# Issuing ScalarE's copy of the row-end column one group of turns sooner

## The chip, the cores and the metric

The kernel runs on one core of a Trainium2 chip. The time is the device time of one execution in microseconds (us); the kernel before has a median of 2385.87 us over three runs (2383.38 to 2386.52). The profile is one further execution, taken by the hardware profiler. Its engines are TensorE (PE, its weight loads PEld), VectorE (DVE), ScalarE (ACT), GpSimd (POOL) and SyncE (SP), which here issues nearly all DMAs.

## The reference, cut to what matters

The input x has 8 images (batches) of 256 channels and 96 x 96 pixels, float32. Two layers are added to it one after the other, each behind a group norm.

```python
def layer0(x):                          # w1, w2, w3, w_out: 256x256, 8 heads of 32 channels
    q, k, v = (fft2(pconv(x, w, b)) for w, b in ((w1, b1), (w2, b2), (w3, b3)))
    q, k = l2_normalize(q), l2_normalize(k)         # over the 9216 frequencies
    attn = einsum('bhcn,bhdn->bhcd', q, k) * temperature
    attn = complex(softmax(real(attn)), softmax(imag(attn)))
    return pconv(abs(ifft2(einsum('bhcd,bhdn->bhcn', attn, v))), w_out)

def layer1(x):                          # q, k: 32 channels, v: 256
    q, k, v = softplus(Wq x + bq), softplus(Wk x + bk), Wv x + bv
    return q (k^T v) / (q . sum(k))     # linear attention over the 9216 pixels

x = x + layer0(gn(x))
x = x + layer1(gn(x))
```

No Fourier transform is needed for the attention's logits. Their real part is a sum over pixels of products of x with itself, and their imaginary part a sum of products of x with x mirrored (row h with row H - h, column w with column W - w). The kernel forms both from the even and odd parts e = f + g and o = f - g, where f is a pixel and g its mirror image.

## The kernel before, in words

The order of work is written out by hand: inside `tc.manual_schedule` every engine executes its instructions in the order in which the program issues them. So an instruction that waits holds up all that stands behind it on its engine.

Each batch goes through these stages. `pair_sums(b)` makes the sums of products of batch b. `attention(b)` makes 36 mixing columns from them. `rotate(b)` transforms rows. `images(b)` makes, for 24 chunks of 384 pixels, the heads' images and projects them into x. `layer1(b)` and `output(b)` are the second layer. The stages of two batches are woven: while `images(b)` works on its last chunks (15 to 23) and `layer1(b)` runs, `pair_sums(b + 1)` is advanced step by step (`weave`). The first sums of batch 0 are made by other code, and its groups 3 to 5 are not woven with images.

In `images`, chunk i takes: the products z on TensorE (L898), an addition of two tables on VectorE (L945), squares on ScalarE (L949), their sum on GpSimd (L950), square roots on ScalarE (L951, and L952 for eight rows of another tile), the projection po of chunk i - 2 on TensorE (L907), its addition to x on VectorE (L909) and two statistics (L313). Every eighth chunk has a few more (L929, L931, L932). Both `images` and `pair_sums` take their working tiles from one ring of five.

`pair_sums` goes over row pairs u = 0 to 12, two of them to a group v = u // 2; a group is one load. Loads alternate between two staging areas (`staged(b, v)`, with index v % 2), each with a part f and a mirrored part g. A turn, `turn_blocks(u)`, makes two 32x32 block transposes on VectorE (L514, one of f and one of g, 128 x 768 each) into `turned(b, u)`, which holds both turns of a group. The columns of g are read backwards from one row's end; the pixel of column 0 has to stand at that end. For this the even turn (r == 0) begins with a copy on ScalarE (L510) that shifts 16 elements on each of the 128 partitions by one row width within g. The second transpose waits for it.

After the odd turn of group v, SP issues two stores of the turned group to DRAM (L520) and the load of group v + 2 into the area that has come free (`load_grouped`, L169 and L171, eight DMAs of 192 KB). The stores read what the turns wrote, and the next group's turns write over it.

`pair(u)` makes the tile eo of e and o from the two transposes: a small memset (L530), the sum (L542, GpSimd) and the difference (L543, VectorE for even u, GpSimd for odd u in batches 1 to 7; pair 0 is made on VectorE). `products` (L475) then runs three sets of matmuls over each eo. During pair u, at its first set, pair u + 1 is made, and at its second set turn u + 2:

```python
if q == 0 and u < NG and u + 1 not in ready:
    prepare(("pair", u + 1), lambda u=u: make(u + 1))
if q == 1 and u + 2 <= NG:
    prepare(("turn", u + 2), lambda u=u: turn_blocks(u + 2))
```

Turns 0 and 1 and pairs 0 and 1 are made together at the start, at chunk 15 of the images. `prepare` runs a step at once, except for turns 10, 11 and 12 and pair 10 in batches 1 to 7: these are held, and `layer1` and `output` release them piece by piece (`release`). `layer1` starts with a group norm: VectorE's L329, ScalarE's L331 and L337, VectorE's L339, with small TensorE products (L128) between, then scaled weights (L975) and the products of L1020.

Of the kernel before, what the change touches and what calls it, by code (L numbers as in the profile page):

```python
# [74 lines left out]
def two_layer_kernel(ctx: ExitStack, tc: tile.TileContext, x, w1t, b1, w2t, b2, w3, b3, wot, temp,  # L75
                     wqt, bq, wkt, bk, wvt, bv, gavg, gmat, tmat, out):
    nc = tc.nc
    B, C, H, W = x.shape
# [11 lines left out]
    NG = H // 2 // G  # L90
# [17 lines left out]
    def x_of(b):  # L108
        return arenas[b % 2]
# [4 lines left out]
    def acc_tile(name):  # L114
        return pacc.tile([P, 512], F32, tag="acc", name=name)

    def ring_tile(name):
        return ring.tile([P, 2 * NQ * (C + 2)], F32, tag="ring", name=name)
# [14 lines left out]
    SG = NB8 * 2 * W  # L133
# [4 lines left out]
    def staged(b, v, at=0):  # L138

        return x_of(b)[:, v % 2, at * SG:at * SG + SG + at]  # L140

    def turned_flat(b, u):

        if b == 0 and u // 2 in (V0 + 1, NG // 2):
            return y_of(b)[:, :, TO2:TO2 + 2 * NQ * C]
        return x_of(b)[:, :, TO:TO + 2 * NQ * C]

    def turned(b, u):

        t = turned_flat(b, u)  # L150
        return [t[:, c].rearrange("p (q r n) -> p q r n", q=NQ, r=2) for c in range(2)]

    def load_grouped(b, v):

        xs = x[b].rearrange("(c i) h w -> i c h w", i=32)
        if 2 * v == NG:
            m = H // 2
            f, g = (staged(b, v, i)[:, 0:C].rearrange("p (c w) -> p c w", c=NB8) for i in range(2))
            for q in range(NQ):
                s = slice(32 * q, 32 * q + 32)  # L160
                n = 32 if q else 31
                o = W + 1 - 32 * (q + 1)
                nc.sync.dma_start(out=f[s], in_=xs[:, :, m, s])
                nc.sync.dma_start(out=g[s, :, 0:n], in_=xs[:, :, m, o:o + n])
            return
        f, g = (staged(b, v, i)[:, 0:SG].rearrange("p (c w) -> p c w", c=NB8) for i in range(2))
        for a in range(G):
            h, s = 2 * (G * v + a), slice(32 * a, 32 * a + 32)
            nc.sync.dma_start(out=f[s], in_=xs[:, :, h:h + 2].rearrange("p c r w -> p c (r w)"))  # L169
            if h:  # L170
                nc.sync.dma_start(out=g[s], in_=xs[:, :, H - h - 1:H - h + 1].rearrange("p c r w -> p c (r w)"))  # L171
            else:
                nc.sync.dma_start(out=g[s, :, 0:W], in_=xs[:, :, H - 1])
                nc.sync.dma_start(out=g[s, :, W:2 * W], in_=xs[:, :, 0])
# [170 lines left out]
    def finish(stage):  # L345
        for _ in stage:
            pass
# [109 lines left out]
    def weights(b):  # L457

        return ring_tile(f"wl_{b}")[:, 0:6 * C].rearrange("p (k o) -> p k o", k=KC)

    def products(acc, eo, q, np_, first, last):
        for c in range(2):
            v = eo[0:np_, q, c]
            for m in range(4):
                if m == 3:
                    to, of = C + 2, bass.AP(v.tensor, v.offset, [list(v.ap[0]), [C - HP + 1, 2], [1, HP + 1]])
                    n = 2 * (HP + 1)
                else:
                    to, n = ((0, 3 * HP + 1), (HP + 1, 3 * HP + 1), (C + 3, P + 1))[m] if not first else ((0, C + 2), (0, C + 2), (C + 2, P + 2))[m]
                    lo = to - (m // 2) * (P + 2)  # L470
                    of = v[:, lo:lo + n]
                o = acc[c][m % 2 * HP:m % 2 * HP + HP, to:to + n]
                if m == 3:
                    o = o.rearrange("p (f n) -> p f n", f=2)
                nc.tensor.matmul(o, lhsT=v[:, 1 + m * HP:1 + (m + 1) * HP], rhs=of, start=(first and m < 2), stop=last,  # L475
                                 skip_group_check=True)

    def pair_sums(b):

        ready = {}  # L480
        u0 = 0 if b else 2 * V0

        def prepare(key, step):
            if b and key in (("turn", 10), ("pair", 10), ("turn", 11), ("turn", 12)):
                held[key] = step()
            else:
                finish(step())

        def make(u):
            ready[u] = pair(u)  # L490
            yield

        acc = [acc_tile(f"acc{c}_{b}") for c in range(2)] if b else s0[0]
        CB = C + 2

        def turn_blocks(u):

            v, r = divmod(u, 2)
            t = turned(b, u)
            if u == NG:  # L500
                f, g = (staged(b, v, i)[0:W, 0:C].rearrange("p (c w) -> p c w", c=NB8) for i in range(2))
                nc.vector.tensor_copy(g[0:32, :, 31:32], f[0:32, :, 0:1])
                for i, src in enumerate((f, g[:, :, ::-1])):
                    nc.vector.transpose(out=t[i][0:W, 0, 0].rearrange("p (c i) -> p c i", c=NB8), in_=src)
                nc.sync.dma_start(out=xtm, in_=t[0][0:W, 0, 0])
                return
            f = staged(b, v, 0).rearrange("p (c r w) -> p c r w", c=NB8, r=2)
            if r == 0:
                g = staged(b, v, 1)
                nc.scalar.copy(g[:, SG:0:-W], g[:, SG - W::-W])  # L510
            o = SG + (1 - r) * W + 1
            g = x_of(b)[:, v % 2, o:o + SG].rearrange("p (c n) -> p c n", c=NB8)[:, :, W - 1::-1]
            for i, src in enumerate((f[:, :, r], g)):
                nc.vector.transpose(out=t[i][:, :, r].rearrange("p q (c i) -> p q c i", c=NB8),  # L514
                                    in_=src.rearrange("p c (q w) -> p q c w", q=NQ))
                if i == 0:
                    yield 1
            if r:
                for c in range(2):
                    nc.sync.dma_start(out=xtd[v][:, :, c], in_=turned_flat(b, u)[:, c].rearrange("p (q m) -> p q m", q=NQ))  # L520
                if v + 2 <= NG // 2:
                    load_grouped(b, v + 2)

        def pair(u):

            eo = ring_tile(f"eo_{b}_{u}").rearrange("p (q c n) -> p q c n", q=NQ, c=2)
            nq, np_ = (NQ, P) if u < NG else (1, W)
            ft, gt = (t[0:np_, 0:nq, u % 2] for t in turned(b, u))
            e, o = (eo[0:np_, 0:nq, c, 1:C + 1] for c in range(2))
            (nc.gpsimd if u < NG else nc.vector).memset(eo[0:np_, 0:nq, :, 0:CB:CB - 1], 1.0 if u < NG else R2)  # L530
            if u == 0:
                nc.gpsimd.memset(eo[0:32, 0:nq, :, 0:CB:CB - 1], R2)
            if u in (0, NG):
                w = R2 if u else pw
                if u:
                    nc.scalar.activation(o, gt, AF.Copy, scale=w)
                else:
                    nc.vector.tensor_scalar_mul(o, gt, w)
                nc.vector.scalar_tensor_tensor(e, in0=ft, scalar=w, in1=o, op0=ALU.mult, op1=ALU.add)
                nc.vector.scalar_tensor_tensor(o, in0=ft, scalar=w, in1=o, op0=ALU.mult, op1=ALU.subtract)  # L540
            else:
                nc.gpsimd.tensor_add(e, ft, gt)  # L542
                (nc.gpsimd if b and u % 2 and u < NG - 1 else nc.vector).tensor_sub(o, ft, gt)  # L543
            return eo, nq, np_

        for step in (turn_blocks(u0), make(u0), turn_blocks(u0 + 1)):
            finish(step)
            if b == 0:
                yield
        finish(make(u0 + 1))  # L550
        yield
        for u in range(u0, NG + 1):
            eo, nq, np_ = ready.pop(u)
            for q in range(nq):
# [4 lines that stand above are left out]
                if (u, q) == (NG - 1, 1):  # L559
                    wl = weights(b)  # L560
                products(acc, eo, q, np_, u == 0 and q == 0, u == NG)
                yield
        s0[b] = acc, wl
# [678 lines left out]
    E = mybir.EngineType  # L1242
    with tc.manual_schedule(engines={E.PE, E.DVE, E.Pool, E.SP, E.Activation}):
        sums, rest, loads, parts = first_sums(), pair_sums(0), first_loads(), tables()
        fetch, turns, tables_to = rotate(0)
        next(loads)
# [81 lines left out]
```

## Time and profile before

| | |
|---|---|
| median of three runs | 2385.87 us |
| the profiled execution | 2381.32 us |
| its span, first to last instruction | 2379.5 us |
| TensorE busy | 2322.5 us, 98% |
| VectorE busy | 1731.4 us, 73% |
| ScalarE busy | 1154.2 us, 49% |
| GpSimd busy | 854.5 us, 36% |
| granted TensorE clock, mean | 0.996 |
| DMA traffic | 405.10 MB, 170 GB/s |
| L510, the copy | 45 times, median 220 ns |
| L514, the transposes | 180 times, median 967 ns |

How to read the lines below. A row of the page's list of groups has the line in the code, the engine and operation, the tiles written and read, the count, then the busy time and the mean duration in ns, and after the bar the idle time of the engine before these instructions, with what ended most of it. A row of the list of waits has who waited for whom, the total in us, how often, and the longest. A row of a timeline has the start and the duration in us, the engine, line, operation, tiles, count (TensorE's counts include its weight loads), and in square brackets the idle time before it and what ended it. An engine with a "q" behind it (DVEq, ACTq, SPq) is that engine's sequencer, which waits and issues.

### The profile page before, as it was taken

To read this page: it belongs to the slowest core of one execution; us is meant where nothing else is said; L and a number is where in the kernel's file an instruction comes from. 1 tells how busy PE (TensorE), PEld (TensorE's weight loads), DVE (VectorE), ACT (ScalarE), POOL (GpSimd) and SP (SyncE) were. 2 spreads that over 40 slices of the span, in tenths; PEclk is the share of its full clock that TensorE was granted. 3 is DMA by queue.
4 is the path that set the end of the run, shared out by engine and by line. 5 is a ranking of instruction groups with operands and counts; after the bars stand their busy time and mean duration, and the time that the engine had idled before them with its cause. 6 is when DMAs were issued, how large, how long until landed. Compare 5 with 4: busy or idle time off the path is not lost. (4 is left out here: it accounts for less than half of the span.)

```text
span 2379.5 us, 62270 instructions
## 1 busy us (share of the span) xinstructions
PE 2322.5 (98%) x26028; PEld 1440.0 (61%) x26028; DVE 1731.4 (73%) x3392; ACT 1154.2 (49%) x2052; POOL 854.5 (36%) x810
## 2 busy tenths in 40 slices
PE   9999999999999999999999999999999999999997
PEld 7844667456674566745666457664676546765444
DVE  5577786777867777677776778767786777876776
ACT  2354454544545355454554535445364453644563
POOL 5234513344223443234341353413524245142412
PEclk9999999999999999999999999999999999999999
DMA  9735749177591666926577364863759538584004
GB/s 252 210 121 145 187 139 331 59 172 174 164 336 41 161 160 203 312 50 159 138 250 264 67 170 132 281 211 67 194 135 292 173 94 195 146 276 179 1 8 160
DMA packets 280346, 405.10 MB, mean 170 GB/s; under 512 B 39363, under 2 KB 202595, under 8 KB 280067
## 3 DMA queue, kind: packets, MB, share of 16 engines
q1 hardware_dynamic: 279714, 401.05, 58.2%
q8 instruction: 206, 3.38, 0.6%
q14 instruction: 74, 0.60, 0.1%
q0 software_dynamic: 352, 0.08, 0.1%
HBM read 251.90 MB, written 149.14 MB: 169 GB/s over the span
## 5 line engine op out<-in xcount | busy, mean ns | idle before, releaser
L898 PE MATMUL z<-arena,mz 128*64 128x384 f32 (+1 forms) x3840 | 593.1, 487 | 0.6 <-issue 0.6
L950 POOL TENSOR_TENSOR e<-e 128x768 f32<-128x768 f32 x192 | 349.3, 1819 | 539.7 <-ACT e L949 513.0
L907 PE MATMUL po<-e,wo 128*64 128x384 f32 x3072 | 529.7, 486 | 2.9 <-ACT e L951 1.7
L898 PEld LDWEIGHTS z<-arena,mz 128*64 128x64 f32 (+1 forms) x3840 | 247.7, 131 | 295.0 <-issue 284.8
L907 PEld LDWEIGHTS po<-e,wo 128*64 128x64 f32 x3072 | 228.2, 137 | 268.6 <-issue 232.2
L945 DVE TENSOR_TENSOR e<-z,xT 128x768 f32<-128x768 f32 x384 | 357.6, 946 | 43.4 <-PE z L898 43.2
L949 ACT ACTIVATE e<-e 128x1536 f32<-128x1536 f32 x192 | 284.4, 1481 | 160.5 <-DVE e L945 158.7
L475 PE MATMUL acc<-eo 128*64 128x193 f32 (+4 forms) x4448 | 341.4, 303 | 13.1 <-POOL eo L542 11.7
L475 PEld LDWEIGHTS acc<-eo 128*64 128x64 f32 (+1 forms) x4448 | 301.4, 136 | 81.5 <-issue 46.7
L951 ACT ACTIVATE e<-e 128x768 f32<-128x768 f32 x192 | 162.0, 844 | 381.5 <-POOL e L950 379.5
L909 DVE TENSOR_TENSOR arena<-arena,po 128x384 f32<-128x384 f32 x384 | 208.0, 549 | 149.9 <-PE po L907 149.8
L128 PE MATMUL y<-tm,arena 96*64 96x97 f32 x6144 | 300.3, 249 | 10.9 <-issue 3.4
L128 PEld LDWEIGHTS y<-tm,arena 96*64 96x64 f32 x6144 | 274.4, 137 | 58.4 <-issue 36.5
L542 POOL TENSOR_TENSOR eo<-arena 128x768 f32<-128x768 f32 x83 | 172.4, 2077 | 345.2 <-DVE arena L514 244.8
L1213 POOL TENSOR_TENSOR arena<-arena,po 128x384 f32<-128x384 f32 x180 | 179.2, 1016 | 279.3 <-ACT po L1212 278.4
L514 DVE STREAM_TRANSPOSE arena<-arena 128x768 f32<-128x768 f32 x180 | 170.2, 962 | 98.6 <-ACT arena L510 83.7
L313 DVE BATCH_NORM_STATS2 st<-arena 128x6 f32<-128x384 f32 x384 | 195.0, 547 | 0.5
L838 ACT COPY arena<-y 128x384 f32<-128x384 f32 (+1 forms) x200 | 94.7, 476 | 155.1 <-PE y L128 141.3
L838 DVE COPY arena<-y 128x384 f32<-128x384 f32 (+1 forms) x192 | 104.1, 543 | 77.2 <-PE y L128 73.7
L1065 PE MATMUL xT<-ident,arena 128*128 128x128 f32 x1152 | 144.1, 275 | 1.3 <-ACT xT L1068 1.3
L1065 PEld LDWEIGHTS xT<-ident,arena 128*128 128x128 f32 x1152 | 127.1, 141 | 19.0 <-issue 16.5
L1212 ACT COPY po<-o 128x384 f32<-128x384 f32 x180 | 80.1, 483 | 101.5 <-PE o L128 87.1
(255 smaller groups left out, 2475.8 us busy)
## 6 DMA issues: line engine op xcount, KB each, us to landing
arena<-in_x_dram SPq DMA_DIRECT2D x99, 768.0 KB
out_dram<-arena SPq DMA_DIRECT2D x192, 384.0 KB
xtd<-arena SPq DMA_DIRECT2D x90, 768.0 KB
arena<-xtd SPq DMA_DIRECT2D x180, 384.0 KB
arena<-in_x_dram SPq DMA_DIRECT2D x353, 192.0 KB
tm<-rx SPq DMA_DIRECT2D x96, 159.0 KB
wl<-in_w1t_dram SPq DMA_DIRECT2D x8, 256.0 KB
wl<-in_w2t_dram SPq DMA_DIRECT2D x8, 256.0 KB
```

What stands on the lines that cost most here:

```text
L128: nc.tensor.matmul(out[h], lhsT=lhsT[:, h], rhs=rhs, start=start, stop=stop, skip_group_check=True)
L313: nc.vector.bn_stats(out=st[:, k, c, :], in_=x_of(b)[:, k, c * CH:(c + 1) * CH])
L475: nc.tensor.matmul(o, lhsT=v[:, 1 + m * HP:1 + (m + 1) * HP], rhs=of, start=(first and m < 2), stop=last, skip_group_check=True)
L838: copy(y[:, :, :, g:g + nr, :], v.rearrange("p k r (f w) -> p k f r w", f=2))
L898: nc.tensor.matmul(out[:, 0:CH].rearrange("p (h q) -> p h q", q=PR), lhsT=columns(mz, k, c, j)[:, h], rhs=yz[:, k, f, :, o:o + PR], start= ...
L907: nc.tensor.matmul(po[h, 0:CH], lhsT=wo[:, k, m * P:(m + 1) * P][:, h], rhs=e[:, k, :], start=(k == 0), stop=(k == KC - 1), skip_group_che ...
L909: nc.vector.tensor_add(x[:, m, n], x[:, m, n], po[:, 0:CH])
L945: nc.vector.tensor_add(e[:, 2 * c:2 * c + 2, :].rearrange("p t (q h) -> p t q h", h=H), pz[:, 0:CH].rearrange("p (h q) -> p q h", h=H).uns ...
L949: nc.scalar.activation(e, e, AF.Square)
L950: nc.gpsimd.tensor_add(e[:, 0:2, :], e[:, 0:2, :], e[:, 2:4, :])
L1065: nc.tensor.transpose(pt[:, j * C + k * P:j * C + (k + 1) * P], x[:, k, o:o + P], ident)
L1213: nc.gpsimd.tensor_add(x[:, m, r], x[:, m, r], t)
```

## The change

The copy gets a function of its own, `turn_round(v)`. It is called for the first group of a batch at the head of its first turn, as before. For each later group it is called at the end of the odd turn of the group before, ahead of that turn's stores and load. The copy itself, the area it works on and what it waits for are the same. It isn't called for the last group (v = 6, one row), which had no such copy before either.

```diff
+        def turn_round(v):
+
+            g = staged(b, v, 1)
+            nc.scalar.copy(g[:, SG:0:-W], g[:, SG - W::-W])
+
         def turn_blocks(u):
 
             v, r = divmod(u, 2)
...
             f = staged(b, v, 0).rearrange("p (c r w) -> p c r w", c=NB8, r=2)
-            if r == 0:
-                g = staged(b, v, 1)
-                nc.scalar.copy(g[:, SG:0:-W], g[:, SG - W::-W])
+            if u == u0:
+                turn_round(v)
             o = SG + (1 - r) * W + 1
...
                 if i == 0:
                     yield 1
+            if r and u + 1 < NG:
+                turn_round(v + 1)
             if r:
                 for c in range(2):
                     nc.sync.dma_start(out=xtd[v][:, :, c], in_=turned_flat(b, u)[:, c].rearrange("p (q m) -> p q m", q=NQ))
```

## The prediction

> **What bounds the kernel now.** I read the page's busy shares first, then the costliest groups. TensorE is busy for 2322.5 of 2379.5 us, so an edit to ScalarE can only pay where TensorE stands still.
>
> ```profile
> span 2379.5 us, 62270 instructions
> PE 2322.5 (98%) x26028; PEld 1440.0 (61%) x26028; DVE 1731.4 (73%) x3392; ACT 1154.2 (49%) x2052; POOL 854.5 (36%) x810
> ...
> L475 PE MATMUL acc<-eo 128*64 128x193 f32 (+4 forms) x4448 | 341.4, 303 | 13.1 <-POOL eo L542 11.7
> ...
> L514 DVE STREAM_TRANSPOSE arena<-arena 128x768 f32<-128x768 f32 x180 | 170.2, 962 | 98.6 <-ACT arena L510 83.7
> ```
>
> VectorE's transposes wait 83.7 us for the copy (L510), but TensorE's own wait in that chain is only 11.7 us. Next I asked for TensorE's waits in one stretch, 475 to 600 us, where the copies of batch 2 run beside the images of batch 1:
>
> ```profile
> PE acc L475 <- POOL eo L542: 1.7, 1, 1.7
> PE po L907 <- DVE arena L909: 0.2, 1, 0.2
> ```
>
> Two waits, 1.67 and 0.16 us, are all above 0.1 us. The same pair is in all seven such stretches (1.83 to 1.87 us each, 12.9 together; batch 0's sums are not woven this way). The timelines of VectorE, ScalarE, GpSimd and TensorE from 508 to 530 us show the chain behind them:
>
> ```profile
> 513.50 0.96 DVE L514 STREAM_TRANSPOSE arena<-arena 128x768 f32<-128x768 f32 x1
> 518.12 0.98 DVE L514 STREAM_TRANSPOSE arena<-arena 128x768 f32<-128x768 f32 x1 [3.67 <-ACT arena L510]
> 519.02 1.78 DVE L945 TENSOR_TENSOR e<-z,xT 128x768 f32<-128x768 f32 x2
> ```
> ```profile
> 516.58 0.84 ACT L951 ACTIVATE e<-e 128x768 f32<-128x768 f32 x1 [3.33 <-POOL e L950]
> 517.46 0.52 ACT L952 ACTIVATE e<-v 8x384 f32<-8x384 f32 x1
> 517.89 0.20 ACT L510 COPY arena<-arena 128x16 f32<-128x16 f32 x1
> ```
> ```profile
> 522.40 1.81 POOL L950 TENSOR_TENSOR e<-e 128x768 f32<-128x768 f32 x1 [5.85 <-ACT e L949]
> 524.15 0.11 POOL L530 MEMSET eo<- 128x12 f32 x1
> 524.34 2.59 POOL L542 TENSOR_TENSOR eo<-arena 128x768 f32<-128x768 f32 x1
> ```
> ```profile
> 524.02 1.29 PE L475 MATMUL acc<-eo 128*64 128x193 f32 x16
> 526.99 1.32 PE L475 MATMUL acc<-eo 128*64 128x193 f32 x16 [1.67 <-POOL eo L542]
> ```
>
> The copy of group 1 stands on ScalarE behind the square roots of image chunk 16 (L951, L952), so the second transpose of turn 2 starts at 518.12. Behind it in VectorE's order stands L945 of chunk 17, then ScalarE's square (L949, 520.84), GpSimd's L950, and behind that, in GpSimd's order, L542 of pair 2, for which TensorE waits. The change acts on this place.
>
> **The change part by part.** It removes and adds no work: 45 copies at 0.22 us before and after. The built order differs on ScalarE alone. In batches 1 to 7 the copies of groups 1 to 5 (35 of the 45) stand earlier; the rest, and the queues of SP (all loads and stores), GpSimd, VectorE and TensorE, are as before.
>
> *Turn 2 (group 1).* The copy now follows that of group 0, at 503.4. Its load landed at 493.8 by the semaphore updates, and ScalarE then stands idle until L931 at 509.57, so it costs nothing. The second transpose does not start at 514.4, when the first ends: VectorE's sequencer also waits there, in the answer for line 514 from 512 to 519 us:
>
> ```profile
> L514 DVEq EVENT_SEMAPHORE  x4: 50/50/2192, 512.7 to 515.2; - x4
> ```
>
> The longest, 2.19 us, ends at 515.12, just after the second store of turn 1 (L520) landed at 515.09: the transpose writes where that store read. So it starts at about 515.3, 2.8 us earlier and not 3.67. In the seven stretches, store against copy, the gain is 2.1 (the one at 1095 us) to 3.0. What follows:
> - L945 of chunk 17: its sums z were made at 510.05 to 512.80, so it moves with the transpose, to 516.2 to 518.0.
> - L949 (1.49): ScalarE is done with L952 at 517.98, so 518.0 to 519.5; before, it began at 520.84.
> - L950 (1.81) then ends at 521.4, and L542 follows the memset. Alone it takes 1.83 (at 509.23); beside VectorE's L543, as here, 2.59. I take 2.59, since the memset releases both again. It ends at 524.1, before 526.93.
> - L909 of chunk 15, for whose PSUM tile TensorE waits 0.16 us at 521.41, starts 2.8 earlier, at 517.9. That wait goes.
> - TensorE then wants pair 2 at 525.31 - 0.16 = 525.15, 1 us after it is ready. In the 1095 us stretch L542 ends at 1104.35 against 1104.66: still in time.
>
> Gain: 1.83 us a stretch, 12.9 over seven. If the chain moved by only part of its 2.8, the bound from below is 0; from above it is the whole wait, 12.9, since no other TensorE wait there hangs on it.
>
> *Turns 4, 6 and 8 (groups 2 to 4).* VectorE's waits of 3.5, 1.9 and 1.8 us shrink; at turns 6 and 8 to about 1.1, because the second stores land at 552.64 and 568.47 and the transposes ran at 553.55 and 569.28. TensorE waits for nothing there, so I count 0. The moved copies can stall ScalarE if the load has not landed. Group 3: landed 541.36, the copy's new place is behind L952 at 547.98. Group 4: landed 560.15, place 561.09, next work 564.19. Group 2: landed 524.25, but its place moves from 525.64 to about 522.8, so it holds ScalarE for 1.4 us. Queued behind it is L949 of chunk 18, which cannot start before L945 of that chunk ends (528.71 before, about 526.0 now); covered by 1.5 us.
>
> *Turn 10 (group 5).* This is the new wait. The copy leaves the next stage's start (585.69) and follows that of group 4, at 569.25. Its load lands at 577.31, so ScalarE is held for 8 us. Behind it stands L331 of the group norm, for which TensorE waits almost at once (released 580.05, used 580.14):
>
> ```profile
> 569.02 0.22 ACT L510 COPY arena<-arena 128x16 f32<-128x16 f32 x1
> 579.85 0.20 ACT L331 ACTIVATE dv_b<-dm_b 128x2 f32<-128x2 f32 x1 [10.60 <-DVE dm_b L329]
> ```
>
> ScalarE was idle there anyhow: L331 starts 2.29 to 3.17 us after the landing in the seven stretches, less 0.22 for the copy. If TensorE brings L331 forward by 1.83 and the load did not move, 0.2 us would be left in the tightest. I expect the load to move too, since turn 7 releases it. Cost 0; the cover is thin.
>
> *Sum.* 7 x (1.67 + 0.17) = 12.9. Profiled: 2381.32 (span 2379.5 and 1.8 around it) to 2368.4. That execution lies 0.2% under the median of the runs, so the forecast is 2385.87 - 12.9 = 2373.0.
>
> **The rivals.**
> 1. *Part of the wait stays.* L542 ends later than I count, for instance because L543 and other VectorE work, now free earlier, stretch it or L950 again by the 0.76 us that parts 2.59 from 1.83. Against it: all 192 of L950 take 1.8, whatever runs beside them. If half the wait stays, 2379.4.
> 2. *The store takes the copy's place.* If the second store of turn 1 lands as late as the copy came (518, not 515.1), VectorE waits for it instead, and nothing moves: 2385.9. The 1095 us stretch, where it landed 2 us later against the transpose, shows that it varies; not by enough.
> 3. *Slower: ScalarE held by group 5's load in front of the group norm.* Each us beyond the cover costs TensorE 7 us; it decides once the load lands 2.1 + 1.83 = 3.9 us later against L331 than now. Were a transfer as long as the two stores (561.62 to 568.47, 6.85 us) in front of it: 7 x (6.85 - 2.1 - 1.83) = 20, so 2406. For it: the thin cover. Against it: the order on SP's queue is unchanged, and seven stretches agree within 0.9 us.
> 4. *TensorE's busy rows hide waits*, and the rest of turn 2's 2.8 us is won too: 7 x 2.8 = 19.6, so 2366.3. Against it: 16 of L907 with their weight loads take 2.75 at 505.06 and at 512.63, and 2.80 beside the disturbed place. The Trainium skill, Perfetto Trace Analysis, section Identifying the Most-Contended Engine, says that matmul busy time is no good measure of how near TensorE is to its limit, because matmuls are pipelined; by that rule this rival would win. These equal rows speak against it here.
>
> **How the numbers follow.** Chances: forecast 0.82, rival 1 0.07, rival 2 0.05, rival 3 0.04, rival 4 0.02. About 0.2% (4.8 us) is what can be told from no change. Faster takes the forecast, rival 4 and most of rival 1: 0.89; same 0.07; slower 0.04. The range goes from the forecast less run scatter (the runs spread over 3 us), 2369.5, to past rival 1, 2381; it leaves out rivals 2 to 4.
>
> **What would show it.** Right: TensorE's waits for L542 and L909 are gone from all seven stretches; the second transpose of turn 2 starts just after the store's landing, about 1.8 us behind the first's start; L510 waits about 8 us for a load once per batch, and L331 still waits for VectorE's L329. Wrong: TensorE's wait in L475 stays with another releaser; or L331 is released by L510, and the second L128 product of the group norm, or L1020, shows idle time.

## The result, and the profile after

The change makes the kernel faster: 2372.66 us (median of four runs, 2369.83 to 2374.33) against 2385.48 us for the kernel before on the same chip (median of four, 2383.38 to 2386.52). The ratio is 0.9946, 95% interval 0.9929 to 0.9963. The forecast was 2373.0 us in a range of 2369.5 to 2381.0.

From here on, line numbers are those of the changed kernel, four to six higher behind the new function: the copy is L499, the transposes L518, the stores L526, the memset L536, the sum and difference of a pair L548 and L549, po L913 and its addition L915, z L904, and the chunk's steps L951 (VectorE), L955 (square), L956 (GpSimd), L957 and L958 (square roots). L475, L331 and L329 keep their numbers.

The page of the changed kernel, its span, busy shares and two groups:

```profile
span 2371.1 us, 62277 instructions
...
PE 2329.3 (98%) x26028; PEld 1456.1 (61%) x26028; DVE 1739.5 (73%) x3392; ACT 1154.5 (49%) x2052; POOL 855.1 (36%) x810
...
L475 PE MATMUL acc<-eo 128*64 128x193 f32 (+4 forms) x4448 | 339.7, 302 | 0.5 <-POOL eo L536 0.5
...
L518 DVE STREAM_TRANSPOSE arena<-arena 128x768 f32<-128x768 f32 x180 | 168.5, 959 | 37.4 <-DMA arena<-in_x_dram 15.2
```

L475's idle time falls from 13.1 to 0.5 us, and the transposes' from 98.6 to 37.4, where the copy no longer leads the causes. In the stretch that the prediction showed, TensorE now waits for nothing at all above 0.1 us, nor in the other six. TensorE's timeline of that place, the kernel before first:

```profile
518.50 2.76 PE L898 MATMUL z<-arena,mz 128*64 128x384 f32 x16
521.41 2.80 PE L907 MATMUL po<-e,wo 128*64 128x384 f32 x16 [0.16 <-DVE arena L909]
...
528.13 2.11 PE L898 MATMUL z<-arena,mz 128*64 128x384 f32 x12
```

and the changed kernel (its stretch begins 4.26 us earlier: the copy of group 0 starts at 498.89, before at 503.15):

```profile
514.23 2.76 PE L904 MATMUL z<-arena,mz 128*64 128x384 f32 x16
516.81 2.76 PE L913 MATMUL po<-e,wo 128*64 128x384 f32 x16
519.39 2.38 PE L475 MATMUL acc<-eo 128*64 128x193 f32 x32
521.58 2.77 PE L904 MATMUL z<-arena,mz 128*64 128x384 f32 x16
```

From z to z it is 9.63 us before and 7.35 after: 2.28 us less, though the two waits that went read only 1.83. Look at the starts: undisturbed, L913 comes 2.58 us after z (516.81 - 514.23), though z's row is 2.76 long. Each row begins 0.17 to 0.2 us before the shown end of the one ahead: the single matmuls of L907 at 512.63 follow each other in pairs 0.32 us apart, but each is shown 0.49 us long (the profile's ends of matmuls are modelled). Before, L907 came 2.91 after z, so 0.33 was lost where the idle column says 0.16. Likewise L475's second set of 16 came 2.97 after its first, where undisturbed sets come 1.10 apart (48 in 515.21 to 518.50): 1.87 lost against 1.67 shown. Both corrections could have been read from the trace of before.

From the start of group 0's copy to the start of L331, over the seven stretches, this gives:

| kernel | the seven stretches, us each | their sum | all the rest of the span |
|---|---|---|---|
| before | 76.69 to 76.72 | 536.9 | 1842.5 |
| changed | 74.41 to 74.54 | 521.1 | 1850.0 |

The saving is 2.27 us a stretch on average, 15.9 in all, and it is the same to 0.05 us in all stretches but one (2.17, the one at 1095 us). What lies outside the stretches, where the change does nothing, was 7.5 us longer in this execution. Nearly all of it stands at two places: the time from one stretch to the next is 2.7 us longer around 1275 and 4.5 us longer around 1852. At each of them TensorE stood still for longer (1.63 us at 1272 and 1.85 us at 1850, where the kernel before shows 0.5), and behind that the granted clock was at half speed, for one and for two pieces of 3.4 us. Half the length of a piece, 1.7 us, is what it can cost, and the experiment with a later load below shows 1.55 to 1.71. From the last stretch on, all takes 1.3 us longer, with two such pieces from 2282 against one at 2294 before. The two pieces at 1852 are in the second line here (the answer by windows: start:end, length, busy time of TensorE, its weight loads, VectorE, ScalarE and GpSimd, granted clock, DMA share, GB/s):

```profile
1848.00:1851.90 3.90, 2.05 (x48) 1.85 (x44) 0.72 (x4) 1.09 (x4) 0.00 (x0) 1.00 1.02 401
1852.00:1858.80 6.80, 6.80 (x97) 4.85 (x96) 2.97 (x13) 0.38 (x2) 0.00 (x0) 0.50 1.03 405
1858.90:1862.00 3.10, 3.10 (x28) 1.18 (x22) 1.45 (x3) 1.05 (x2) 1.44 (x2) 1.00 1.03 402
```

Other traces of the changed kernel lack these pieces at 1275 and 1852, and some with TensorE's old waits have such pieces elsewhere, so they are no part of the change. These two places are also why the spans of the two profiled executions differ by only 8.4 us.

The chain behind the gain, engine by engine. VectorE's timeline of the changed kernel:

```profile
509.25 0.96 DVE L518 STREAM_TRANSPOSE arena<-arena 128x768 f32<-128x768 f32 x1
510.97 0.98 DVE L518 STREAM_TRANSPOSE arena<-arena 128x768 f32<-128x768 f32 x1 [0.76 <-issue]
511.87 1.78 DVE L951 TENSOR_TENSOR e<-z,xT 128x768 f32<-128x768 f32 x2
```

GpSimd's:

```profile
515.25 1.81 POOL L956 TENSOR_TENSOR e<-e 128x768 f32<-128x768 f32 x1 [2.93 <-ACT e L955]
517.00 0.11 POOL L536 MEMSET eo<- 128x12 f32 x1
517.19 2.60 POOL L548 TENSOR_TENSOR eo<-arena 128x768 f32<-128x768 f32 x1
```

and ScalarE's, at the copies of groups 2 and 5:

```profile
519.85 0.22 ACT L499 COPY arena<-arena 128x16 f32<-128x16 f32 x1 [1.36 <-DMA arena<-in_x_dram]
521.60 1.48 ACT L955 ACTIVATE e<-e 128x1536 f32<-128x1536 f32 x1 [1.52 <-DVE e L951]
...
570.87 0.22 ACT L499 COPY arena<-arena 128x16 f32<-128x16 f32 x1 [8.50 <-DMA arena<-in_x_dram]
573.32 0.20 ACT L331 ACTIVATE dv_b<-dm_b 128x2 f32<-128x2 f32 x1 [2.22 <-DVE dm_b L329]
```

The second transpose starts 1.72 us behind the first, held for 0.76 us by VectorE's sequencer and no longer by the copy. By the semaphore updates turn 1's second store lands at 510.79, and the sequencer's wait ends at 510.82. GpSimd's L548 ends at 519.79, and TensorE's second set, the first that reads it, starts at 520.49. ScalarE waits 8.50 us for group 5's load, ends the copy at 571.09, and is idle for another 2.22 us until VectorE releases L331.

### The profile page after: what moved, and what is told of

Same layout as the page of the kernel before. It is cut to its first block, busy times and chain, and to the rows that moved or that the text cites. A ratio compares the mean times of both kernels' runs of the same rounds, so it can differ in the third digit from the quotient of the medians.

```text
span 2371.1 us, 62277 instructions
## 1 busy us (share of the span) xinstructions
PE 2329.3 (98%) x26028; PEld 1456.1 (61%) x26028; DVE 1739.5 (73%) x3392; ACT 1154.5 (49%) x2052; POOL 855.1 (36%) x810
## 5 line engine op out<-in xcount | busy, mean ns | idle before, releaser
L904 PE MATMUL z<-arena,mz 128*64 128x384 f32 (+1 forms) x3840 | 596.4, 490 | 0.2 <-issue 0.2
L956 POOL TENSOR_TENSOR e<-e 128x768 f32<-128x768 f32 x192 | 349.6, 1821 | 542.4 <-ACT e L955 515.7
L913 PE MATMUL po<-e,wo 128*64 128x384 f32 x3072 | 530.0, 486 | 1.8 <-ACT e L957 1.8
L904 PEld LDWEIGHTS z<-arena,mz 128*64 128x64 f32 (+1 forms) x3840 | 250.6, 132 | 295.1 <-issue 274.3
L951 DVE TENSOR_TENSOR e<-z,xT 128x768 f32<-128x768 f32 x384 | 360.9, 949 | 60.8 <-PE z L904 60.2
L913 PEld LDWEIGHTS po<-e,wo 128*64 128x64 f32 x3072 | 232.0, 137 | 262.3 <-issue 221.6
L955 ACT ACTIVATE e<-e 128x1536 f32<-128x1536 f32 x192 | 284.4, 1481 | 140.4 <-DVE e L951 138.7
L957 ACT ACTIVATE e<-e 128x768 f32<-128x768 f32 x192 | 162.0, 844 | 381.8 <-POOL e L956 379.8
L475 PEld LDWEIGHTS acc<-eo 128*64 128x64 f32 (+1 forms) x4448 | 303.2, 136 | 65.0 <-issue 45.0
L475 PE MATMUL acc<-eo 128*64 128x193 f32 (+4 forms) x4448 | 339.7, 302 | 0.5 <-POOL eo L536 0.5
L915 DVE TENSOR_TENSOR arena<-arena,po 128x384 f32<-128x384 f32 x384 | 209.2, 551 | 169.8 <-PE po L913 169.8
L548 POOL TENSOR_TENSOR eo<-arena 128x768 f32<-128x768 f32 x83 | 172.7, 2080 | 327.0 <-DVE arena L518 225.2
L518 DVE STREAM_TRANSPOSE arena<-arena 128x768 f32<-128x768 f32 x180 | 168.5, 959 | 37.4 <-DMA arena<-in_x_dram 15.2
L1071 PEld LDWEIGHTS xT<-ident,arena 128*128 128x128 f32 x1152 | 127.1, 141 | 19.0 <-issue 16.5
```

The costliest lines, as they stand in the source:

```text
L904: nc.tensor.matmul(out[:, 0:CH].rearrange("p (h q) -> p h q", q=PR), lhsT=columns(mz, k, c, j)[:, h], rhs=yz[:, k, f, :, o:o + PR], start= ...
L913: nc.tensor.matmul(po[h, 0:CH], lhsT=wo[:, k, m * P:(m + 1) * P][:, h], rhs=e[:, k, :], start=(k == 0), stop=(k == KC - 1), skip_group_che ...
L915: nc.vector.tensor_add(x[:, m, n], x[:, m, n], po[:, 0:CH])
L951: nc.vector.tensor_add(e[:, 2 * c:2 * c + 2, :].rearrange("p t (q h) -> p t q h", h=H), pz[:, 0:CH].rearrange("p (h q) -> p q h", h=H).uns ...
L955: nc.scalar.activation(e, e, AF.Square)
L956: nc.gpsimd.tensor_add(e[:, 0:2, :], e[:, 0:2, :], e[:, 2:4, :])
```

## The experiments

My theory: the whole gain is TensorE's two waits at turn 2, so it comes from the copy of group 1 alone; the copies of groups 2 to 5 move and bring nothing; and the new wait for group 5's load is hidden by 2.1 to 3 us of ScalarE's idle time before the group norm. The rivals: the gain comes from the later turns' shorter VectorE waits, or from the start of the next stage, from which group 5's copy was taken away; and the early copies cost something that a larger gain covers. Later the size of the gain came up as well, as 2.27 us a stretch do not stand in the waits. Stretches are those of the table above.

### Group 1 alone, groups 2 to 4 alone, group 5 alone

Three kernels take the change for some of the groups only. The edit, with `early` as (1,), (2, 3, 4) or (5,):

```diff
-            if r == 0:
-                g = staged(b, v, 1)
-                nc.scalar.copy(g[:, SG:0:-W], g[:, SG - W::-W])
+            if u == u0 or r == 0 and v not in early:
+                turn_round(v)
...
+            if r and u + 1 < NG and v + 1 in early:
+                turn_round(v + 1)
```

> Only the copy of group 1 is issued early; those of groups 2 to 5 stand where they stood before. Theory (the whole gain is TensorE's wait for pair 2, which hung on this copy): 12.9 us under the kernel before, ratio 0.9946, the same time as the full change within 2 us, and no wait of L475 for L548 in the seven stretches. Rival (the earlier copies of groups 2 to 4 win part of it, hidden in TensorE's busy rows): clearly less than the full change, by 3 us or more.

> Only the copies of groups 2, 3 and 4 are issued early; that of group 1 stays behind the square roots of chunk 16. Theory: no change from the kernel before (within 2 us, ratio 0.999 to 1.001), although VectorE's waits at turns 4, 6 and 8 shrink; TensorE still waits 1.7 us for L548 in each of seven stretches. Rival (those waits count): 3 us or more faster than before.

> Only the copy of group 5 is issued early, in front of the group norm, where it waits some 8 us for its load. Theory (covered): no change from the kernel before, within 2 us, and L331 is still released by VectorE's L329. Rival (the early copy holds ScalarE up there): slower, by 7 us for every us that L331 is late.

Group 1 alone: 2370.25 us against 2387.66, ratio 0.9931 (0.9916 to 0.9946). Six stretches take 74.42 to 74.43 us and one 74.74, and TensorE's two waits are gone. Groups 2 to 4 alone: 2386.35 us, 0.9998 (0.9988 to 1.0008), stretches of 76.69 to 76.77. Group 5 alone: 2385.72 us, 0.9993 (0.9984 to 1.0002), stretches of 76.69 to 76.72. With groups 2 to 4 early, the list of TensorE's waits from 470 to 600 us is still that of before:

```profile
PE acc L475 <- POOL eo L548: 1.7, 1, 1.7
PE po L913 <- DVE arena L915: 0.2, 1, 0.2
```

With group 5 early, ScalarE's timeline has the long wait and, behind it, the group norm released by VectorE as before:

```profile
567.32 0.22 ACT L499 COPY arena<-arena 128x16 f32<-128x16 f32 x1
575.64 0.22 ACT L499 COPY arena<-arena 128x16 f32<-128x16 f32 x1 [8.11 <-DMA arena<-in_x_dram]
578.13 0.20 ACT L331 ACTIVATE dv_b<-dm_b 128x2 f32<-128x2 f32 x1 [2.27 <-DVE dm_b L329]
```

So one of five moved copies carries the whole gain, and the 8 us wait is free. This was the forecast, and the two rivals on where the gain comes from fall.

### The changed kernel again, twice, and the kernel before against itself

No edit.

> The changed kernel itself, beside the three parts on the same chip: 12.8 us under the kernel before, ratio 0.9946. If the parts add up, its gain is the sum of theirs: 12.9 + 0 + 0.

> The changed kernel once more, since it gained 12.8 us in one comparison and 19.3 in another. Theory (the work of the change is the 13.4 us of TensorE's waits that the profiles show gone; the rest is scatter of the half-clock stretches): 10 to 18 us under the kernel before. Rival (there is a second effect of 6 us): 19 us again.

> The kernel before against itself, to see what a comparison tells: ratio 1.000 within 0.0015, and 1.7 us waits of L475 for L542 in seven stretches. If the earlier gain of 19 us on one chip came from something in the kernel before that the first profile does not show (half-clock stretches after its 1.7 us gaps), they stand in this profile behind those gaps.

The changed kernel: 2368.39 us against 2387.66, ratio 0.9918 (0.9906 to 0.9931), and on another chip 2369.46 against 2386.18, 0.9926 (0.9909 to 0.9943). The kernel before against itself on that chip: 1.0002 (0.9991 to 1.0014). Its stretches take 76.70 to 76.75 us, those of the changed kernel 74.41 to 74.44 in both runs. No half-speed piece stands behind its seven waits of 1.7 us.

The three comparisons of medians give 12.8, 19.3 and 16.7 us, and group 1 alone gave 17.4. The stretches give 15.9 to 16.2, and this lies in the intervals of the first and the third; the second, in us 16.5 to 22.4, just leaves it out. The stretches are the better measure of what the change does, since they hold to a few hundredths where runs of one kernel differ by some 10 us. Why the second comparison read more is not settled; whether the clock's half-speed pieces were merely fewer in those four executions wasn't tried.

### The changed kernel without the early copies

```diff
-            if r and u + 1 < NG:
+            if r and u + 1 < NG and b == 0:
                 turn_round(v + 1)
```

> The changed kernel without the copies of groups 1 to 5 in batches 1 to 7 at all (35 of 45; column 0 of their mirrored rows is then taken from the wrong place, which the sums of products take in). Theory (issued early, the copies cost nothing any more): the same time as the changed kernel, within 2 us. Rival (they still cost, by ScalarE's 8 us wait in front of the group norm or otherwise): 3 us or more faster.

2372.22 us against 2386.18, ratio 0.9930 (0.9914 to 0.9946); stretches of 74.40 to 74.43, one of 74.56. The changed kernel beside it had 2369.46, so the medians lie 2.8 us apart, a little more than expected and against the rival's direction; the seven stretches add up to 521.1 and 520.9 us. With the copies gone altogether it is no faster than the change. The rival that they cost something falls. Nothing is left to win at these copies either.

### A later load for group 5

The new wait's cover, put to the test: eight more stores of 256 KB, into a scratch tensor that nothing reads, stand ahead of group 5's load on SP's queue; once in the changed kernel and once in the kernel before. In the changed kernel:

```diff
             if r and u + 1 < NG:
                 turn_round(v + 1)
...
+                if b and v == 3:
+                    for n in range(8):
+                        nc.sync.dma_start(out=junk[n], in_=wo.rearrange("p k o -> p (k o)"))
```

> The changed kernel with eight extra stores of 256 KB (a constant tile to an unused DRAM tile) on SP's queue in front of the load of group 5, once in each of batches 1 to 7; they hold up that load's landing by some 5 us (2.1 MB at the 390 GB/s that the stores reach). Theory (the early copy of group 5 has only 2.1 to 3.0 us of cover before L331, after which each us costs TensorE 7 us over the batches): L331 2 to 3 us late in each, released by the copy or the load, TensorE idle there, and 12 to 22 us slower than the changed kernel, so about as slow as the kernel before or slower. Rival (TensorE finds other work, the cover does not matter): as fast as the changed kernel.

> The kernel before with the same eight stores in the same place. Its copy of group 5 stands behind the group norm, 8.4 us after the load's landing. Theory: within 3 us of the kernel before, so that what the stores cost the changed kernel is the early copy's wait. Rival (the stores themselves slow the kernel, by traffic or by holding up SP's queue): as much slower as in the changed kernel.

In the changed kernel: 2397.87 us against 2387.34, ratio 1.0042 (1.0024 to 1.0059), so the gain is gone and more. In the kernel before: 2386.70, 0.9997 (0.9985 to 1.0009), so the stores themselves cost nothing. The changed kernel with them, ScalarE first (L500 is the copy, L332 the group norm's step):

```profile
579.96 0.22 ACT L500 COPY arena<-arena 128x16 f32<-128x16 f32 x1 [13.56 <-DMA arena<-in_x_dram]
580.09 0.20 ACT L332 ACTIVATE dv_b<-dm_b 128x2 f32<-128x2 f32 x1
```

and TensorE:

```profile
580.34 0.28 PE L128 MATMUL gv_b<-dv_b,gavg_sb 128*64 128x2 f32 x4 [2.49 <-ACT dv_b L332]
```

Against group 0's copy the copy of group 5 starts 5.1 us later than without the stores (77.0 against 72.0 us). Of these, the cover takes 2.2, and the stretch is 2.74 longer (77.17 against 74.43). The seven stretches add up to 539.5 us, 18.4 more than in the changed kernel. The medians, each against the kernel before beside it, say 23 to 30 more (+10.5 against -12.8 to -19.3), over the 12 to 22 expected. Most of the rest comes from the clock. Behind six of the seven stalls stands a piece of 3.4 us at half speed. The seventh shows what it costs: there TensorE is 600 matmuls behind the start of the group norm's step L332 after 49.30 us, and in the six others after 50.85 to 51.01, so a piece loses 1.55 to 1.71 us, some 10 in all. The answer by windows, with the columns as above, where the clock of 0.50 is to be seen and the full one behind it:

```profile
582.10:585.50 3.40, 3.40 (x33) 1.32 (x27) 0.16 (x1) 1.79 (x4) 0.00 (x0) 0.50 0.96 225
585.50:589.00 3.50, 3.50 (x48) 1.56 (x44) 1.77 (x4) 2.67 (x5) 0.00 (x0) 1.00 0.95 257
```

This is rival 3, brought about by the stores. It is a real mechanism, and what keeps it away is only the landing of one load, 2.1 us ahead of need in the tightest stretch.

### Three more copies on ScalarE, ahead of the copy of group 1 or of group 2

In the kernel before, the copy of one group is made 1.8 us later still, by three copies into a part of a tile that is not in use there. With `late` as 1 or 2:

```diff
             if r == 0:
+                if b and v == late:
+                    for _ in range(3):
+                        nc.scalar.copy(xT[:, 3, :, 0:C], sel8.unsqueeze(1).to_broadcast([P, 2, C]))
                 g = staged(b, v, 1)
```

> The kernel before with three ScalarE copies of 512 elements (some 0.6 us each) into an unused tile in front of the copy of group 1, in batches 1 to 7: that copy comes about 1.8 us later. Theory (its delay goes into TensorE's wait one to one): the wait of L475 grows from 1.7 to about 3.5 us and the kernel is 7 x 1.8 = 12.6 us slower than before. Rival (other links of the chain also bind, or slack takes it up): less than half of that.

> The kernel before with the same three ScalarE copies in front of the copy of group 2 instead. VectorE then waits 1.8 us longer at turn 4, but pair 4 is ready 6 us before TensorE uses it (L542 ends at 543.08, first used at 549.09). Theory: no change, within 2 us. Rival (any wait of VectorE for the copy costs the same): 12.6 us slower.

Group 1: 2400.34 us against 2387.34, ratio 1.0067 (1.0045 to 1.0089); the stretches take 78.51 to 78.54, 12.8 us more in all. The size is as expected (12.6): with no slack left, what the copy loses TensorE loses in full. The place is not. TensorE's waits in that stretch (po is L910 here, its addition L912, the sum L545):

```profile
PE po L910 <- DVE arena L912: 2.0, 1, 2.0
PE acc L475 <- POOL eo L545: 1.7, 1, 1.7
```

The wait for the sum stays at 1.67. It is the small wait of 0.16 us at po that grew, to 1.99: the addition L912 stands behind the same late transpose in VectorE's order, and TensorE meets it first. TensorE is then late itself, so the sum is no later for it than before. The two waits are one delay, met at two places.

Group 2: 2390.57 us, 1.0022 (1.0011 to 1.0033), stretches of 77.51 to 77.77, 6.3 us more in all where I had expected none. VectorE's wait at turn 4 grew from 3.48 to 5.31 us, and TensorE's wait at pair 4 did not appear. But TensorE waits for L912 once more, much later:

```profile
PE acc L475 <- POOL eo L545: 1.7, 1, 1.7
PE po L910 <- DVE arena L912: 0.8, 2, 0.6
```

One of these two is the old 0.2 us; the other, 0.63 us, comes at 573.18, some 31 us after the transpose. Set beside the kernel before, each from its copy of group 0 on, the two traces show what carries the delay so far. The second transposes of turns 4, 6 and 8 start 1.87, 1.89 and 1.88 us later, and so do ScalarE's copies of groups 3 and 4, for which the last two wait. TensorE falls behind for the first time at this wait, by 0.87 us, and stays so. So the delay runs round between ScalarE and VectorE undiminished until it meets an addition that TensorE needs. The slack behind turn 4 is about 1 us of 1.8 (1.83 less the 0.90 lost in each stretch), and not the 6 us that pair 4 itself has. Groups 2 to 4 bring nothing when earlier, and group 2 costs when it is later: the kernel before stood close to the edge there. Groups 3 and 4 were not made later.

## Why the prediction was right, point by point

- **What bounds the kernel.** Right. The whole gain is TensorE's idle time at one place, and an edit that saves VectorE 61 us of waiting saves the kernel 16.
- **Turn 2.** Right in each step, in the stretch at 500 us set back to the old time by 4.26: the second transpose was to start at about 515.3 (510.97, so 515.23), L956 to end at 521.4 (521.32), L548 to take 2.59 and end at 524.1 (2.60, 524.05). That the store's landing would hold the transpose, so that only 2.8 of its 3.67 us go, was right too: 0.76 us remain, and the store lands 0.03 us before the sequencer's wait ends. TensorE was to find pair 2 ready for 1 us; it is 0.7, since TensorE gets there 0.4 us sooner than reckoned, for the reason under *Sum*.
- **Both waits gone in all seven stretches**, the one at 1095 us among them: right.
- **Turns 4, 6 and 8**: counted at 0, and 0 was measured. VectorE's own waits came out a little otherwise: about 1.1 us was to be left at turns 6 and 8, and at turn 6 nothing is left in six stretches (1.20 in the other), at turn 8 0.9 to 1.0 in six (1.89 in the other). Group 2's copy was to hold ScalarE for 1.4 us under a cover of 1.5: it holds it for 1.36, and 1.52 are left. The reason "TensorE waits for nothing there" hides that the slack behind turn 4 is only about 1 us.
- **Turn 10.** Right: the copies wait 7.7 to 8.6 us for group 5's load, L331 still waits for L329, and 2.14 to 2.98 us of cover are left. The load moved with turn 7, as I expected. Had it not, nothing would be left in the tightest stretch: the 0.2 us of the prediction reckon with 1.83, and each stretch became shorter by 2.17 or more, which is over the 2.07 (2.29 - 0.22) of cover there.
- **Sum.** Here a term was mis-sized. "7 x (1.67 + 0.17) = 12.9" takes the idle column for the time lost. Each stretch gives 2.27, 15.9 in all, since a matmul row's shown end lies 0.17 to 0.2 us behind the point at which the next row would start, and so each wait of the list is that much too short. From 2381.32 this would have given 2365.4 in place of 2368.4, and from the median 2370.0 in place of 2373.0. That the first comparison came out at 12.8 us, next to 12.9, is in part luck, the scatter of executions: the repeats gave 19.3 and 16.7, with medians of 2368.39 and 2369.46, just under the range's lower edge of 2369.5.
- **Rivals.** 1 (part of the wait stays), 2 (the store takes its place) and 3 (group 5's load) did not come; the 0.76 us are what there is of 2. Rival 3 exists and has a price of 2.2 to 3.0 us a stretch, and more by the clock, once the load is 5.1 us later, as the experiment shows. Rival 4 said that TensorE's rows hide waiting, and I dismissed it by rows of L907 that took 2.75 and 2.80 us. That looked at the lengths of the rows, and what hides the waiting is their overlap. It did not win: 2.27 us a stretch is not its 2.8, though it lies nearly half of the way there from 1.83. But the rule that I set beside it (the Trainium skill, Perfetto Trace Analysis, section Identifying the Most-Contended Engine: matmul busy time misleads, since matmuls are pipelined) holds on a small scale: 0.44 of 2.27 us stood inside busy time. The busy total is no guide either: in the trace shown it rose from 2322.5 to 2329.3 us while the kernel became faster, and in the two further traces of the changed kernel it is 2321.7 and 2323.3. I put the rise down to the half-speed pieces, in which every row is longer.

One more correction. The text before the result says that TensorE's counts include its weight loads, and the prediction speaks of 16 of L907 "with their weight loads". They do not: PE and PEld are counted apart (26028 each on the page), and the 16 are matmul rows, two for each of the eight float32 products.

## What to carry to other kernels

Cost a wait on TensorE from start to start of the same rows, in a disturbed and in an undisturbed place of the same trace, and not by the idle column: here two waits that read 1.83 us cost 2.27. Where a step is moved up in a queue that is written out by hand, look at each place for what TensorE wants next: one copy of five was worth all 16 us, though VectorE's waits fell at four turns. And a long new wait is free as long as its end stays ahead of need, so note the margin: here it is 2.1 us, and a transfer that delays the load by 5 us turns the gain into a loss.

## What the runs showed of the hardware that I had not expected

**Short gaps can halve TensorE's clock.** In the experiment with the later load, six of the seven gaps of 2.06 to 2.68 us at the group norm were followed by a piece of 3.4 us at a granted clock of 0.5. The Trainium skill (TensorE: Matmul & The Clock Gate, section Why this matters for your kernels) advises no idle gaps over about 3 us; here gaps well below that were enough. The Trainium skill (TensorE: Matmul & The Clock Gate, Part 1, What's actually happening) says that the clock is judged in windows of 3413 ns that run freely, and the trace agrees: the six pieces start at 288.5, 582.1, 872.2, 1165.8, 1749.4 and 2039.6 us, all a whole number of 3.413 us apart (86, 85, 86, 171 and 85). So where a gap falls matters. Laid on the grid of these starts, the six gaps leave TensorE idle for 1.68 to 2.68 us of one window. The seventh, though 2.56 us long, falls across a boundary, with 1.07 us in one window and 1.49 in the next, and it went free.

The idle time in a window is not the whole rule, though. Gaps of 1.67 us (1.66 to 1.69) at pair 2 had no such piece behind them, in all 42 stretches of six traces (two of the kernel before, and four of kernels that keep this wait), although up to 1.69 us fell into one window. Of the seven gaps of 1.99 us, with three more copies ahead of group 1's, one had a piece behind it, and another had none with 1.96 us in one window. And outside the stretches, in the middle of the kernel, a piece stood behind gaps of only 0.80 to 1.20 us in three traces (the parts with group 1 and group 5 alone, and the kernel without the early copies), while most gaps of that length had none. What else counts is open.

**The scatter between executions of one program** is of the same make in part: outside the seven stretches the traces of all kernels differ by up to 14 us, while the stretches themselves repeat to a few hundredths. In the trace of the changed kernel that is shown above, the two places with an idle gap and a half-speed piece behind it account for 7.2 of the 7.5 us. It is not all: the first repeat of the changed kernel has a trace with no such piece between 80 us and 2270 us, and the rest of its span is still 4.1 us longer than in the kernel before. At the very end, from 2340 us, the clock was at half speed for 33 us against 13 before, and yet all from the last stretch on, the two pieces at 2282 included, took only 1.3 us longer (352.3 against 351.0): a slower clock costs little where TensorE isn't the bound.
